# VectorE's column copies begin four steps behind ScalarE's

## The chip, the cores and the metric

The kernel runs on one core of one Trainium2 chip. The time is the device time of one execution in microseconds; the median of the runs counts. Engines: PE is TensorE, DVE is VectorE, ACT is ScalarE, POOL is GpSimd, SP is SyncE (it only issues transfers here).

## What is computed

One layer of a graph network with 12500 nodes of 64 features and 200000 edges, which are sorted by target:

```python
nodes = concat(x[src], x[dst])                       # per edge, 128 features
gates = (ssp(edge_attr @ We1 + be1) @ We2 + be2) * soft_cutoff(distance)
h = ssp(nodes @ Wn1 + bn1) @ Wn2 + bn2
message_sum = zeros_like(x).at[dst].add(h * gates)
x = layernorm(2 * x + ssp(message_sum @ Ws1 + bs1) @ Ws2 + bs2)
```

`ssp(x)` is softplus less log 2.

## The kernel before

**Steps.** The edges are cut into 391 steps of 512 (NG tiles `xg`, each with four parts of 128 edges, one edge per partition). Iteration i of the main loop is written out by hand as one order per engine:

- SP loads edge features (`eT`, every second step) and two windows of rows of a table of target features (`wns`) for step i+5.
- POOL gathers the source rows of step i+3: one indirect transfer per part of 128 rows (L204), four per step, into one of eight buffers `xg`. The gather after the eighth has to wait until PE's scatter of the buffer's former step is done, so POOL's group for a step starts on a signal of PE.
- PE: bias of layer 1 (L299) and layer 2 (L342), the scatter of step i-2 (L371, a product with one-hot columns), the transposes of step i+1 (L286), the edge part of layer 1 (L304), its node part (L311), and then layer 2 of step i (L349, L354).
- ACT copies the transposed tile (`xT`, L294), which L311 needs, then does columns (below), exp (L325) and log (L328).
- DVE adds the scatter's two windows to the sums (L391), multiplies `h` (L363) and the message (L367), takes the softplus' other half (L333), makes the one-hot columns of step i+3 (L280), and then does columns.

In a step whose gather group (of step i+5) has four parts, PE also does a product that nobody reads (L337, from `four`), before it waits for ACT's copy.

**Slots.** A copy of x lies transposed in SBUF (`xh`). For some of the parts of 128 edges, called slots, the source rows aren't gathered: an engine copies the column of each of the 128 sources (L262, 4 bytes in each partition), 16 in each step, into a tile `column`. DVE has queue 0 and part 1 of its tile, ACT queue 1 and part 2. After eight steps a tile is whole. `choose` then merges it on DVE: two instructions (L274) take the half of the partitions that holds the source, and PE adds the result to layer 1 with two products (L314) two steps later. In the `xg` of a slot's step the part is set to zero by DVE (L202, in iteration g-3, ahead of the windows), and POOL has three gathers instead of four. `slots_by_columns` places the slots: the first step that leaves enough steps for the copies and has no slot in the step before or behind; ACT's slots are placed first. `read_columns` loads 16 places into registers (L245) in each step; `columns` also has SP broadcast the slot's sources (`side`, L259) in the first of its eight steps.

**Node blocks.** When all edges of 512 nodes have been added (a first block of 212 nodes and 24 of 512; `block_steps` fixes the step from the shares of edges), the block's part is done beside the main loop, one piece per step: L410 is its first product. It stands in PE's order behind layer 2 of its iteration, reads the sums, and so waits for DVE's windows of that iteration; what DVE does after them is L425 and L426. Most blocks have L410 two iterations behind their step (`BLOCK_STEPS`): iterations 55, 98, 127, 151, 171, 189, 205, 220, 234, 247, 260, 272, 283, 294, 305, 315, 325, 334, 344, 353, 361, 370, 378, 386; the last block is done behind the loop.

## Time and profile before

| | us |
|---|---|
| median of 3 runs | 2354.7 (2352.55 to 2364.48) |
| profiled execution | 2351.35 |
| its span, first to last instruction | 2349.3 |
| mean granted clock of TensorE | 0.964 |
| DVE's column copies (6016) | 486.4 |
| ACT's column copies (6016) | 608.8 |
| merges L274 (188) | 53.5 |
| POOL's gathers L204 (1469) | 1391.3 |

A row of the page's groups gives the line, the engine, the operation, output and inputs, the shape, the count, then busy time and the mean of one in ns, and the idle time of the engine just before with what ended it. A row of the table of waits reads: who waited, for whom; microseconds in total, times, longest. A row of a timeline gives start, duration, engine, line, operation, operands and count, and in brackets the idle time before it and its releaser. A row of a stretch gives its limits and length, busy time and count of PE, PE's weight loads, DVE, ACT and POOL, the granted clock, and DMA share and rate.

### The profile page before, as it was taken

Reading aid. Unit: us, or ns where it says so; the run is one execution under the profiler, and the core shown is the slowest. Engines: PE = TensorE matmul, PEld = TensorE weight load, DVE = VectorE, ACT = ScalarE, POOL = GpSimd, SP = SyncE. Lnnn points to the kernel's source line nnn. Section 1 sums busy time; section 2 is a strip of 40 time slices with the busy share of each in tenths; the row PEclk is TensorE's granted clock in tenths of the full one; section 3 lists DMA queues with packets and bytes.
Section 4 is the critical chain, followed back from the end, with each engine's and each line's share of the span. In section 5 each row is a group of like instructions: output and inputs, shape, how many; then the busy total and the mean of one; then the engine's idle time right before and its main releaser. Section 6 shows DMA issues by size and latency. Waiting matters only on the chain.

```text
span 2349.3 us, 49245 instructions
## 1 busy us (share of the span) xinstructions
PE 1986.8 (85%) x12011; PEld 1549.9 (66%) x12011; DVE 1536.7 (65%) x9110; ACT 1511.8 (64%) x7412; POOL 1391.5 (59%) x1473
## 2 busy tenths in 40 slices
PE   6788888888888888888888888888888888888877
PEld 4676666666666666666666666666666666666665
DVE  4467666666666666666666667666666676667655
ACT  3466667666666666666667667666666666666653
POOL 6556666566666566666656566665666665556550
PEclk8799999999999999999999999999999999999988
DMA  6332232322222222222222222222222222222220
GB/s 190 95 83 71 64 70 57 79 62 74 60 59 57 54 62 54 59 56 61 55 58 63 52 61 63 59 59 58 59 59 59 59 61 60 55 56 59 60 51 13
DMA packets 162385, 149.51 MB, mean 64 GB/s; under 512 B 40564, under 2 KB 112021, under 8 KB 161962
## 3 DMA queue, kind: packets, MB, share of 16 engines
q1 hardware_dynamic: 114650, 96.55, 15.1%
q0 software_dynamic: 47008, 48.23, 10.9%
q8 instruction: 101, 1.65, 0.3%
q14 instruction: 192, 1.57, 0.2%
q10 hardware_dynamic: 434, 1.50, 0.2%
HBM read 136.50 MB, written 9.62 MB: 62 GB/s over the span
## 4 chain that ended last, share of the span: by engine, by line
PE 76%; issue 12%; DVE 6%; ACT 2%; DVEq 2%; another core or an unknown queue 1%; DMA 1%; POOL 0%; ACTq 0%; POOLq 0%
PE z L311 17%; PE gh L354 13%; PE z L371 10%; PE tx L286 9%; PE gh L349 8%; PE z L304 6%; PE z L337 4%; PE gh L342 3%; PE z L299 3%; DVE column L262 2%; DVEq L245 2%; ACT xT L294 1%; PE tx L410 1%; PE z L314 1%
## 5 line engine op out<-in xcount | busy, mean ns | idle before, releaser
L204 POOL DMA_INDIRECT xg<-in_x,src_i x1469 | 1391.3, 947 | 905.6 <-PE tx L286 378.3
L294 ACT COPY xT<-tx 106x512 f32<-106x512 f32 x391 | 228.6, 585 | 736.1 <-PE tx L286 704.6
L311 PE MATMUL z<-xT,wns 106*128 106x256 f32 x1564 | 464.1, 416 | 270.5 <-issue 238.0
L262 ACT COPY column<-xh 128x4 uint8 x6016 | 608.8, 193 | 0.0
L311 PEld LDWEIGHTS z<-xT,wns 106*128 106x128 f32 x1564 | 273.8, 197 | 420.4 <-issue 336.4
L262 DVE COPY column<-xh 128x4 uint8 x6016 | 486.4, 199 | 11.9 <-issue 6.9
L363 DVE TENSOR_TENSOR h<-gh,cut 128x256 f32<-128x256 f32 x391 | 166.0, 425 | 380.3 <-PE tx L286 260.8
L354 PE MATMUL gh<-consts,s 128*128 128x64 f32 x3128 | 400.2, 272 | 0.0
L354 PEld LDWEIGHTS gh<-consts,s 128*128 128x128 f32 x3128 | 389.6, 196 | 0.1
L328 ACT ACTIVATE u<-u,one 128x768 f32<-128x768 f32 x392 | 365.8, 933 | 13.5 <-ACT u L325 0.8
L333 DVE SCALAR_TENSOR_TENSOR s<-u,z 128x768 f32<-128x768 f32 x392 | 369.3, 942 | 0.4 <-issue 0.3
L391 DVE TENSOR_TENSOR sums<-sums,z 64x42 f32 x778 | 149.4, 192 | 325.5 <-issue 243.1
L325 ACT ACTIVATE u<-z 128x768 f32<-128x768 f32 x392 | 314.7, 803 | 47.2 <-PE z L311 25.5
L371 PEld LDWEIGHTS z<-xg,msg 128*128 128x128 f32 x1556 | 208.9, 195 | 140.9 <-issue 123.4
L371 PE MATMUL z<-xg,msg 128*128 128x84 f32 x1556 | 269.9, 297 | 13.6 <-DVE msg L367 13.5
L349 PEld LDWEIGHTS gh<-consts,s 128*128 128x128 f32 x1564 | 218.8, 196 | 92.7 <-DVE s L333 68.3
L349 PE MATMUL gh<-consts,s 128*128 128x128 f32 x1564 | 269.8, 296 | 11.8 <-issue 7.2
L286 PE MATMUL tx<-consts,xg 128*106 128x128 f32 x1564 | 243.9, 280 | 0.0
L304 PE MATMUL z<-eT,consts 128*128 128x256 f32 x782 | 243.7, 395 | 0.0
L286 PEld LDWEIGHTS tx<-consts,xg 128*106 128x106 f32 x1564 | 187.1, 145 | 1.2 <-issue 1.2
L367 DVE TENSOR_TENSOR msg<-gh,h 128x256 f32<-128x256 f32 x391 | 165.9, 424 | 13.4
L342 PE MATMUL gh<-row,ones 3*128 3x512 bf16 x391 | 149.3, 382 | 0.0
(107 smaller groups left out, 1193.4 us busy)
## 6 DMA issues: line engine op xcount, KB each, us to landing
eT<-in_eT SPq DMA_DIRECT2D x195, 256.0 KB
xg<-in_x,src_i POOLq DMA_INDIRECT x1469
wns<-table SPq DMA_DIRECT2D x782, 21.0 KB
table<-tb SPq DMA_DIRECT2D x14, 448.0 KB
side<-in_sides SPq DMA_DIRECT2D x94, 64.0 KB
y<-in_x SPq DMA_DIRECT2D x24, 128.0 KB
out<-y SPq DMA_DIRECT2D x24, 128.0 KB
xh<-in_xh SPq DMA_DIRECT2D x2, 781.5 KB
```

Source lines behind the costliest of these rows:

```text
L204: behind(note(("gather", g), nc.gpsimd.indirect_dma_start(out=xg[:, k, :D], out_offset=None, in_=x, in_offset=bass.IndirectOffsetOnAxis(ap ...
L262: copy(column_tiles[slot].bitcast(U8)[:, 4 * r : 4 * r + 4], xh[:, bass.ds(column_at[queue][j] - xh_at, 4)])
L286: ins = nc.tensor.transpose(tx[:, k, :], xgs[g][:, k, :DW], ident)
L294: note(("xcopy", g), nc.scalar.copy(xT, xTs[g]))
L304: nc.tensor.matmul(zs[g][:, 0, :HE], we1.rearrange("a h d -> a (h d)"), eTs[g], start=False, stop=True, skip_group_check=True)
L311: nc.tensor.matmul(zn, wns[:, g % REST, h, :], xTs[g][:, h], start=True, stop=not chosen, skip_group_check=True)
L325: nc.scalar.activation(us[g][:, part], z_of(g)[:, part], AF.Exp)
L328: nc.scalar.activation(us[g][:, part], us[g][:, part], AF.Ln, bias=one)
L333: nc.vector.scalar_tensor_tensor(ss[g].rearrange("p i t e -> p (i t e)")[:, part], us[g][:, part], BIG, z_of(g)[:, part], OP.min, OP.max)
L349: nc.tensor.matmul(v[:, 0, t], ss[g][:, 0, t, :], we2, start=False, stop=False, skip_group_check=True)
L354: nc.tensor.matmul(ghs[g][:, 1, 2 * t + h, :], ss[g][:, 1 + h, t, :], wn2, start=False, stop=h == 1 and t == 1, skip_group_check=True)
L371: ins = nc.tensor.matmul(sc, msgs[g][:, 2 * t : 2 * t + 2, :].rearrange("p h f -> p (h f)"), xgs[g][:, 2 * t : 2 * t + 2, D:DW], start=t = ...
```

## The change

Where the copies begin becomes a pair, for DVE and for ACT. ACT's still begin in iteration 8, DVE's in iteration 12 instead of 8.

```diff
-COLUMNS_FROM = 8
+COLUMNS_FROM = (12, 8)
...
-            if (g - 3 - COLUMNS_FROM + 1) * columns >= (n + 1) * P and not {g - 1, g, g + 1} & taken:
+            if (g - 3 - COLUMNS_FROM[queue] + 1) * columns >= (n + 1) * P and not {g - 1, g, g + 1} & taken:
...
-        return len(own[queue]) * P - columns_done[queue] if i >= COLUMNS_FROM else 0
+        return len(own[queue]) * P - columns_done[queue] if i >= COLUMNS_FROM[queue] else 0
```

ACT's 47 slots stay at steps 18, 26, ... 386. DVE's were at 20, 28, ... 388 (47) and are now at 22, 30, ... 382 (46). DVE's tiles become whole in iterations 19, 27, ... (remainder 3 of 8) instead of 15, 23, ... (remainder 7), where ACT's still do. The zeroing L202 of DVE's slots moves from iterations of remainder 1 to remainder 3. The rows below are in each engine's program order.

DVE, from message 167 to the windows of iteration 168 (remainder 0), before:

```order
L367 TENSOR_TENSOR msg<-gh,h 128x256
L333 TENSOR_SCALAR s<-u,z 128x768
L280 TENSOR_TENSOR xg<-consts,rel 128x4x42
L245 TENSOR_LOAD columns_at
L262 COPY column_24233<-xh 128x4 x16
L274 TENSOR_SCALAR chosen_25313<-side_24127,column_24126 64x128 x2
L274 TENSOR_SCALAR chosen_25316<-side_24234,column_24233 64x128 x2
L391 ISA
L391 TENSOR_TENSOR sums<-sums,z 64x42
```

and now (the two rows of L274 were the merges of ACT's and of DVE's slot):

```order
L367 TENSOR_TENSOR msg<-gh,h 128x256
L333 TENSOR_SCALAR s<-u,z 128x768
L280 TENSOR_TENSOR xg<-consts,rel 128x4x42
L245 TENSOR_LOAD columns_at
L262 COPY column_24638<-xh 128x4 x16
L274 TENSOR_SCALAR chosen_25118<-side_23929,column_23928 64x128 x2
L391 ISA
L391 TENSOR_TENSOR sums<-sums,z 64x42
```

ACT's merges stand alone there now; DVE's stand four iterations later, at the same place of the row.

DVE, from the columns of iteration 170 to the windows of iteration 171, a block's iteration (L410 on PE waits for these windows), before:

```order
L280 TENSOR_TENSOR xg<-consts,rel 128x4x42
L245 TENSOR_LOAD columns_at
L262 COPY column_25446<-xh 128x4 x16
L391 ISA
L391 TENSOR_TENSOR sums<-sums,z 64x42
```

and now:

```order
L280 TENSOR_TENSOR xg<-consts,rel 128x4x42
L245 TENSOR_LOAD columns_at
L262 COPY column_24638<-xh 128x4 x16
L202 MEMSET xg 128x64
L391 ISA
L391 TENSOR_TENSOR sums<-sums,z 64x42
```

The zeroing of a slot's part has come ahead of the windows.

DVE, from the columns of iteration 219 to the windows of iteration 220, another block's, before:

```order
L280 TENSOR_TENSOR xg<-consts,rel 128x4x42
L245 TENSOR_LOAD columns_at
L262 COPY column_32807<-xh 128x4 x16
L391 ISA
L391 TENSOR_TENSOR sums<-sums,z 64x42
```

and now, with the two merges of DVE's slot ahead of the windows:

```order
L280 TENSOR_TENSOR xg<-consts,rel 128x4x42
L245 TENSOR_LOAD columns_at
L262 COPY column_31990<-xh 128x4 x16
L274 TENSOR_SCALAR chosen_33085<-side_31991,column_31990 64x128 x2
L391 ISA
L391 TENSOR_TENSOR sums<-sums,z 64x42
```

Nothing else on DVE's row has moved between these rows.

## The prediction

> **What bounds the kernel now.** I read the page first, then the table of waits, then the timeline of POOL and of ACT's xT copy over a few steps.

> ```profile
> span 2349.3 us, 49245 instructions
> PE 1986.8 (85%) x12011; PEld 1549.9 (66%) x12011; DVE 1536.7 (65%) x9110; ACT 1511.8 (64%) x7412; POOL 1391.5 (59%) x1473
> ACT xT L294 <- PE tx L286: 704.6, 364, 9.8
> POOL xg L204 <- PE tx L286: 378.3, 284, 3.4
> ```

> No engine is full. ACT's copy waits for the transposes in nearly every step (364 waits of 391, 1.9 us each), POOL in most (284), and PE's layer 1 needs that copy. So the kernel is a ring of waits, and its length has to be read from single steps. POOL's gathers, then the xT copies of the same stretch:

> ```profile
> 1002.88 0.94 POOL L204 DMA_INDIRECT xg<-in_x,src_i  x1 [0.91 <-PE tx L286]
> ...
> 1006.63 0.94 POOL L204 DMA_INDIRECT xg<-in_x,src_i  x1 [0.30 <-issue]
> 1008.91 0.94 POOL L204 DMA_INDIRECT xg<-in_x,src_i  x1 [1.33 <-PE tx L286]
> ...
> 1013.55 0.94 POOL L204 DMA_INDIRECT xg<-in_x,src_i  x1 [1.21 <-PE tx L286]
> ...
> 1019.59 0.94 POOL L204 DMA_INDIRECT xg<-in_x,src_i  x1 [1.35 <-PE tx L286]
> ```

> ```profile
> 1008.73 0.58 ACT L294 COPY xT<-tx 106x512 f32<-106x512 f32 x1 [2.19 <-PE tx L286]
> 1013.44 0.58 ACT L294 COPY xT<-tx 106x512 f32<-106x512 f32 x1 [0.93 <-PE tx L286]
> 1019.41 0.59 ACT L294 COPY xT<-tx 106x512 f32<-106x512 f32 x1 [2.20 <-PE tx L286]
> 1025.46 0.58 ACT L294 COPY xT<-tx 106x512 f32<-106x512 f32 x1 [2.27 <-PE tx L286]
> ```

> A group of four gathers lasts 6.03 us from its start to the next group's (1002.88 to 1008.91), a group of three, which is a step whose tile has a slot, 4.64 (1008.91 to 1013.55). The copies come in the same rhythm: 4.71, 5.97, 6.05. The last gather ends 1.16 us before the copy (1006.63 + 0.94 to 1008.73). Thus **a step's length is set by how many gathers POOL has in it**, 4 or 3, and each slot is worth about 1.39 us. DVE's and ACT's column copies and the merges lie inside these steps.

> **The change part by part.**

> *Slots.* ACT's stay where they are (tiles 18, 26, 34 ... 386, 47 of them). DVE's go from 20, 28 ... 388 (47) to 22, 30 ... 382 (46). Every eight steps still hold two groups of three and six of four, now four apart. Their sum doesn't change: 2 x 4.7 + 6 x 6.0 either way. A group that is ready early gains nothing either, since POOL's first gather of a group waits for PE in every step above. What is lost is the slot of tile 388. Its group of three is the one that starts at 2279.54, in the last dozen steps, where a step is longer:

> ```profile
> 2279.54 0.94 POOL L204 DMA_INDIRECT xg<-in_x,src_i  x1 [3.38 <-PE z L371]
> ```

> ```profile
> 2271.68 0.59 ACT L294 COPY xT<-tx 106x512 f32<-106x512 f32 x1 [0.16 <-PE tx L286]
> 2280.16 0.58 ACT L294 COPY xT<-tx 106x512 f32<-106x512 f32 x1 [4.70 <-PE tx L286]
> 2285.97 0.58 ACT L294 COPY xT<-tx 106x512 f32<-106x512 f32 x1 [1.85 <-PE tx L286]
> ```

> With four gathers that step took 8.48 (2271.68 to 2280.16), with three 5.81. So the lost slot costs 1.4 (mid-kernel) to 2.7 us (here); I take the nearer row, **+2.7**.

> *Merges.* Four of them stood together, at the end of DVE's every eighth step:

> ```profile
> 1022.33 0.58 DVE L274 SCALAR_TENSOR_TENSOR chosen<-side,column 64x128 f32<-64x128 int32 x2
> 1023.82 0.59 DVE L274 SCALAR_TENSOR_TENSOR chosen<-side,column 64x128 f32<-64x128 int32 x2 [0.91 <-DVE chosen L274]
> 1024.55 0.19 DVE L391 TENSOR_TENSOR sums<-sums,z 64x42 f32 x1
> 1025.26 0.20 DVE L391 TENSOR_TENSOR sums<-sums,z 64x42 f32 x1 [0.52 <-issue]
> 1025.49 0.42 DVE L363 TENSOR_TENSOR h<-gh,cut 128x256 f32<-128x256 f32 x1
> ```

> They take 2.08 us with their gap (1022.33 to 1024.41), the windows follow, and h starts at 1025.49, when PE's signal for it had come at the latest (ACT's copy, which waits for a later PE instruction, starts at 1025.46). That step is 6.05 long, no longer than its neighbours: the merges just fit under the gathers, and if they grew, the cover would be gone. Halving them frees about 1 us of DVE that nothing waits for. Only the step behind a short one may gain: 5.97 where DVE is on time, 6.05 with DVE late. That is at most 0.08 in each of 46 rounds of eight, -3.7 us, and at least 0; I take the middle, **-2**.

> *DVE's copies.* 128 copies, 2 merges and 8 register loads fewer on DVE, 4 matmul rows fewer on PE, one gather more:

> ```profile
> L262 DVE COPY column<-xh 128x4 uint8 x6016 | 486.4, 199 | 11.9 <-issue 6.9
> ```

> 128 of the 6016 copies are 10.3 us of DVE time (486.4 / 47), all of it beside gathers: 0, and at best the 0 to 1 us that DVE might be late with in the last steps. The side tiles' transfers on SP's queue are the same, now in two steps of eight; SP issues them behind the step's own loads, and no wait of the table is for them: 0.

> *Where the moved pieces meet a node block.* This is the one place where DVE's lateness is paid. PE's first matmul of a block (L410) stands before the step's scatter and transposes and waits for DVE's windows; whatever DVE has in front of those windows, a memset of a slot's tile or the merges, delays PE. Three such meetings: without either, with a memset, behind four merges.

> ```profile
> 1041.06 1.10 PE L410 MATMUL tx<-sums,consts 128*128 128x256 f32 x4 [0.20 <-issue]
> ```

> ```profile
> 923.45 0.11 DVE L202 MEMSET xg<- 128x64 f32 x1
> 923.49 0.13 DVE L391 TENSOR_TENSOR sums<-sums,z 64x42 f32 x1
> 924.87 0.20 DVE L391 TENSOR_TENSOR sums<-sums,z 64x42 f32 x1 [1.26 <-issue]
> ```

> ```profile
> 925.22 1.10 PE L410 MATMUL tx<-sums,consts 128*128 128x256 f32 x4 [1.54 <-DVE sums L391]
> ...
> 1625.52 1.36 PE L410 MATMUL tx<-sums,consts 128*128 128x256 f32 x4 [1.77 <-DVE sums L391]
> ```

> ```profile
> 920.52 0.58 ACT L294 COPY xT<-tx 106x512 f32<-106x512 f32 x1 [0.92 <-PE tx L286]
> 928.84 0.58 ACT L294 COPY xT<-tx 106x512 f32<-106x512 f32 x1 [4.55 <-PE tx L286]
> ...
> 1620.56 0.59 ACT L294 COPY xT<-tx 106x512 f32<-106x512 f32 x1 [2.03 <-PE tx L286]
> 1629.59 0.58 ACT L294 COPY xT<-tx 106x512 f32<-106x512 f32 x1 [5.26 <-PE tx L286]
> ```

> Alone, PE waits 0.20 us. Behind a memset the second window stalls 1.26, PE waits 1.54, and the step is 8.32 long (920.52 to 928.84), 2.3 over a step of four gathers. Behind four merges PE waits 1.77 and the step is 9.03 (1620.56 to 1629.59), 3.0 over. Part of that is the clock: after the stall the granted clock of TensorE falls.

> ```profile
> 922.90:926.30 3.40, 1.86 (x12) 1.36 (x12) 0.92 (x11) 1.36 (x2) 1.89 (x2) 1.00 0.20 43
> 926.50:929.90 3.40, 3.40 (x14) 2.83 (x13) 3.37 (x18) 1.06 (x8) 1.37 (x2) 0.50 0.06 16
> ```

> With PE busy for 1.86 of 3.40 us, the next 3.4 us ran at 0.50 of full speed. [...]

> Now the counting, with the blocks' plan laid beside the slots (a block's first matmul stands two steps behind the step that its edges are complete in, which the code fixes). A block's first matmul stands at steps 171, 283, 315 (remainder 3 of 8), where a memset now comes in front; at 305 and 361 (remainder 1), where it goes away; at 220 and 260 (remainder 4), where two merges now stand in front; at 272 and 344 (remainder 0), where four become two. So three meetings begin and two end at a memset, price 0 to 2.3, I take 1.4, near the middle: net +1.4. Two begin at two merges, 0 to 3.0, I take 0.8 (half of the 1.57 by which PE's wait behind four merges, 1.77, is over the clean 0.20): +1.6. Two shrink by as much: -1.6. Blocks that meet a short step lose its gain: four did, four do. Sum **+1.4**, an estimate from these rows, with ends of -7.8 (two memsets gone at 2.3 each, two blocks relieved by 1.6 each) and +12.9 (3 x 2.3 + 2 x 3.0).

> Sum: 2.7 - 2 + 1.4 = +2.1 us against the profiled execution's 2351.35 (span 2349.3), 2353.5. The median of the runs shown, 2354.7, lies 3.35 above that execution, so as a median I expect 2354.7 + 2.1 = **2357**, to the microsecond. A measurement of this kernel can tell some 0.5% (12 us) from no change.

> **The rivals.**

> *Only the lost slot counts.* The steps are bound by gathers, everything else is covered: +1.4 to +2.7, 2356 to 2357. For it: merges and copies wait for nothing in most steps. It ends where the forecast does.

> *Slower: the moved pieces trip the clock at node blocks.* Place: PE's L410 at steps 171, 283, 315 (memset) and 220, 260 (merges). Price: if each costs as much as the worst quoted, the 12.9 above, with nothing given back at the others, and +2.7: 2354.7 + 15.6 = 2370. It decides once DVE's second window ends so late that PE stands for about 1.5 us, as in the row of 925.22; 0.20 costs nothing. For it: DVE had no slack there (924.87). Against: the same number of such meetings goes away.

> *Faster: four merges in one step were what made DVE late.* Behind them stands the 9.03 step, and DVE's rows from 1022.33 show it just in time. If halving saves the 3.0 at both blocks of remainder 0 and at one more place like them (-9.0), all of the -3.7, and nothing begins elsewhere, the sum is 2.7 - 12.7 = -10, 2345; with a whole stall of 2.3 saved elsewhere too, 2342. Against: most rounds show no cost.

> *The spacing itself gains.* If POOL could use the four steps between short groups to run ahead, 30 gathers of 1.25 us (1.24 from start to start inside a group) would need 37.5 us where eight steps take 45.7. Every group's start waits for PE, 1.2 to 1.35 us after the gather before, so I give this almost nothing: it would be 2354.7 - 8.2 x 46 = 1977.

> **How the numbers follow.** Forecast 0.45 and only the lost slot 0.29, both within 0.5%; clock trips 0.15, all of it beyond 0.5%; relief 0.10, half of it below 2343, which is 0.5% under the median; running ahead 0.01. Range: the ends of the three terms are 1.4 - 3.7 - 7.8 = -10 and 2.7 + 0 + 12.9 = +16, 2344 to 2370; cut by the rarer half of each side, 2346 to 2368. Slower by over 0.5% (above 2366.5): 0.15; faster 0.05 + 0.01 = 0.06; same the rest, 0.79.

> **What would show it.** Groups of three gathers of 4.64 us four steps apart, groups of four still 6.03; the step of 8.48 / 5.81 at the end twice near 8.5; L274 in pairs with no late h; PE's waits for DVE's windows at L410 up at the three blocks with a memset in front, down at 305 and 361. I am wrong if a group of four gets shorter or longer than 6.0, or if the granted clock falls in more than two or three stretches that are new.

## The result, and the profile after

| | before | after |
|---|---|---|
| median, runs of both on one chip | 2355.76 us (22 runs) | 2368.12 us (22 runs) |
| ratio of the times, 95% interval | | 1.005 [1.0035, 1.0064] |
| profiled execution | 2351.35 us | 2367.95 us |
| its span | 2349.3 us | 2366.2 us |
| mean granted clock of TensorE | 0.964 | 0.962 |

The change made the kernel slower by 0.35 to 0.64%, 12.4 us between the medians. I had forecast +2.1 us. By the ratio this is 2366.5 us on the prediction's base of 2354.7, inside the range of 2346 to 2368; the median itself, 2368.12, stands on the range's upper edge. So about 10 us are to be explained. First the changed kernel's page and two rows of its table of waits:

```profile
span 2366.2 us, 49082 instructions
PE 1993.2 (84%) x12011; PEld 1554.2 (66%) x12011; DVE 1528.2 (65%) x8979; ACT 1516.5 (64%) x7412; POOL 1397.0 (59%) x1474
ACT xT L294 <- PE tx L286: 708.4, 367, 10.3
POOL xg L204 <- PE tx L286: 381.7, 284, 4.7
```

The work of the engines is the same within 9 us, and each of the two waits grew by less than 4 us in total. The averages don't show the loss, so I went back to single steps. POOL's group starts in the changed kernel, from its timeline:

```profile
604.40 0.95 POOL L204 DMA_INDIRECT xg<-in_x,src_i  x1 [1.34 <-PE tx L286]
...
610.48 0.94 POOL L204 DMA_INDIRECT xg<-in_x,src_i  x1 [1.38 <-PE tx L286]
...
616.52 0.94 POOL L204 DMA_INDIRECT xg<-in_x,src_i  x1 [1.35 <-PE tx L286]
...
621.16 0.95 POOL L204 DMA_INDIRECT xg<-in_x,src_i  x1 [1.20 <-DVE sums L391]
```

Groups of four last 6.08 and 6.04 us, a group of three 4.64 (616.52 to 621.16). An undisturbed round of eight steps costs what it did before. I call a step with three gathers short and one with four long. ACT's xT copies cut the whole span into stretches; these are the copies that begin steps 19, 94, 376 and 390, before:

```profile
154.89 0.59 ACT L294 COPY xT<-tx 106x512 f32<-106x512 f32 x1 [2.18 <-PE tx L286]
...
587.29 0.59 ACT L294 COPY xT<-tx 106x512 f32<-106x512 f32 x1 [0.94 <-PE tx L286]
...
2233.03 0.58 ACT L294 COPY xT<-tx 106x512 f32<-106x512 f32 x1 [1.78 <-PE tx L286]
...
2326.94 0.59 ACT L294 COPY xT<-tx 106x512 f32<-106x512 f32 x1
```

and after:

```profile
155.11 0.59 ACT L294 COPY xT<-tx 106x512 f32<-106x512 f32 x1 [1.91 <-PE tx L286]
...
598.22 0.59 ACT L294 COPY xT<-tx 106x512 f32<-106x512 f32 x1 [0.90 <-PE tx L286]
...
2251.72 0.59 ACT L294 COPY xT<-tx 106x512 f32<-106x512 f32 x1 [2.37 <-PE tx L286]
...
2343.07 0.59 ACT L294 COPY xT<-tx 106x512 f32<-106x512 f32 x1
```

| stretch | before | after | difference |
|---|---|---|---|
| to step 19 | 154.9 | 155.1 | +0.2 |
| steps 19 to 93 (the table's chunks are made beside) | 432.4 | 443.1 | **+10.7** |
| steps 94 to 375 | 1645.7 | 1653.5 | +7.8 |
| steps 376 to 389 | 93.9 | 91.4 | -2.6 |
| step 390 to the end of the span | 22.4 | 23.1 | +0.8 |

The differences add up to the 16.9 us between the spans. (That is more than the 12.4 between the medians: the profiled execution of before was 4.4 us faster than its median, that of after stood at its median.) Most of it lies in a stretch that the prediction didn't look at and that holds one node block. There the changed kernel has short steps that are no longer short. Step 65 is one; the copies that begin steps 64 to 67, and the granted clock in stretches around it:

```profile
423.61 0.59 ACT L294 COPY xT<-tx 106x512 f32<-106x512 f32 x1 [1.51 <-PE tx L286]
429.74 0.59 ACT L294 COPY xT<-tx 106x512 f32<-106x512 f32 x1 [2.19 <-remote]
437.62 0.59 ACT L294 COPY xT<-tx 106x512 f32<-106x512 f32 x1 [3.20 <-PE tx L286]
443.61 0.59 ACT L294 COPY xT<-tx 106x512 f32<-106x512 f32 x1 [0.82 <-PE tx L286]
```

```profile
427.00:430.20 3.20, 1.79 (x13) 1.53 (x12) 1.17 (x5) 1.01 (x3) 1.47 (x3) 1.00 0.51 139
430.30:433.70 3.40, 3.32 (x12) 2.96 (x12) 3.30 (x24) 2.73 (x19) 2.46 (x3) 0.50 0.19 39
433.80:440.40 6.60, 6.60 (x26) 5.41 (x26) 4.02 (x25) 2.73 (x19) 2.79 (x3) 0.50 0.26 66
```

PE was busy for 1.79 of 3.20 us, then ran for 10 us at a granted clock of 0.50 (a dip, from here on). Step 65 has three gathers and lasted 7.88 us (429.74 to 437.62), 3.2 too long, and the long step behind it gave almost nothing back (5.99). Before the change there were dips in this stretch as well. Here is one in the long step 75 of the kernel before, copies and stretches:

```profile
478.69 0.58 ACT L294 COPY xT<-tx 106x512 f32<-106x512 f32 x1 [2.15 <-PE tx L286]
484.90 0.58 ACT L294 COPY xT<-tx 106x512 f32<-106x512 f32 x1 [1.54 <-PE tx L286]
490.75 0.58 ACT L294 COPY xT<-tx 106x512 f32<-106x512 f32 x1 [1.90 <-PE tx L286]
```

```profile
476.00:479.30 3.30, 2.11 (x14) 1.54 (x13) 1.48 (x7) 1.15 (x5) 1.58 (x3) 1.00 0.12 22
479.40:482.80 3.40, 3.40 (x13) 3.04 (x13) 2.31 (x19) 2.72 (x17) 2.49 (x4) 0.50 0.14 32
```

That dip of 3.4 us made a step of 6.21 and one of 5.85, nothing in sum: at full clock PE stands still for 1.15 us of a long step (4.89 busy of 6.04 in this row of the changed kernel), and the slow products run into that time.

```profile
610.30:616.34 6.04, 4.89 (x30) 3.73 (x30) 3.54 (x24) 3.75 (x19) 3.78 (x4) 1.00 0.30 72
616.34:621.04 4.70, 4.06 (x27) 3.35 (x28) 3.75 (x24) 3.75 (x19) 2.84 (x3) 1.00 0.16 35
```

A short step leaves 0.64 (4.06 of 4.70). Counted over steps 19 to 375 from the records of the granted clock, the dips didn't become more frequent (18 before, 16 after; 85 and 99 us in all). What changed is where they lie: 3.6 us of the half-speed time were in short steps before, 53.4 are now.

About half of the 10.7 us lies in one place, steps 24 and 25. These copies begin steps 24, 25 and 26 after the change:

```profile
184.05 0.59 ACT L294 COPY xT<-tx 106x512 f32<-106x512 f32 x1 [2.13 <-PE tx L286]
192.14 0.59 ACT L294 COPY xT<-tx 106x512 f32<-106x512 f32 x1 [4.15 <-remote]
200.02 0.59 ACT L294 COPY xT<-tx 106x512 f32<-106x512 f32 x1 [2.28 <-PE tx L286]
```

The two steps take 8.09 and 7.88 us, together 5.2 over the medians of their kinds; before the change they were 0.4 under. PE stood for 3.43 us ahead of its layer 1 at 192.78, and a dip of 10.2 us that began at 191.34 lay on step 25, which is now short. Every trace with slots four apart but that of the last run has this stop (2.4 to 5.9 us over the two steps), and none with slots two apart (-0.4 to 0.0). What starts it isn't known.

### The profile page after: what moved, and what is told of

It reads as the page before. It is cut to its first block, busy times and chain, and to the rows that moved or that the text cites. A ratio compares the mean times of both kernels' runs of the same rounds, so it can differ in the third digit from the quotient of the medians.

```text
span 2366.2 us, 49082 instructions
## 1 busy us (share of the span) xinstructions
PE 1993.2 (84%) x12011; PEld 1554.2 (66%) x12011; DVE 1528.2 (65%) x8979; ACT 1516.5 (64%) x7412; POOL 1397.0 (59%) x1474
## 4 chain that ended last, share of the span: by engine, by line
PE 73%; issue 12%; DVE 5%; ACT 2%; DVEq 2%; another core or an unknown queue 0%; ACTq 0%
PE z L311 16%; PE gh L354 12%; PE z L371 9%; PE tx L286 8%; PE gh L349 8%; PE z L304 6%; PE z L337 3%; PE gh L342 3%; PE z L299 3%; DVEq L245 2%; DVE column L262 1%; PE tx L410 1%; ACT xT L294 1%; DVE h L363 1%; PE z L314 1%
## 5 line engine op out<-in xcount | busy, mean ns | idle before, releaser
L204 POOL DMA_INDIRECT xg<-in_x,src_i x1470 | 1396.7, 950 | 917.0 <-PE tx L286 381.7
L294 ACT COPY xT<-tx 106x512 f32<-106x512 f32 x391 | 229.3, 586 | 750.1 <-PE tx L286 708.4
L262 ACT COPY column<-xh 128x4 uint8 x6016 | 612.3, 195 | 0.0
L262 DVE COPY column<-xh 128x4 uint8 x5888 | 476.0, 198 | 11.9 <-issue 7.5
L363 DVE TENSOR_TENSOR h<-gh,cut 128x256 f32<-128x256 f32 x391 | 166.1, 425 | 405.2 <-PE tx L286 328.9
L328 ACT ACTIVATE u<-u,one 128x768 f32<-128x768 f32 x392 | 366.6, 935 | 12.7
L391 DVE TENSOR_TENSOR sums<-sums,z 64x42 f32 x778 | 149.7, 192 | 344.9 <-issue 228.5
L371 PEld LDWEIGHTS z<-xg,msg 128*128 128x128 f32 x1556 | 209.0, 195 | 141.3 <-issue 124.3
L371 PE MATMUL z<-xg,msg 128*128 128x84 f32 x1556 | 269.8, 297 | 13.1 <-DVE msg L367 11.5
L286 PE MATMUL tx<-consts,xg 128*106 128x128 f32 x1564 | 243.4, 280 | 0.0
L286 PEld LDWEIGHTS tx<-consts,xg 128*106 128x106 f32 x1564 | 186.5, 145 | 0.9 <-issue 0.9
```

What stands on the lines that cost most here:

```text
L204: behind(note(("gather", g), nc.gpsimd.indirect_dma_start(out=xg[:, k, :D], out_offset=None, in_=x, in_offset=bass.IndirectOffsetOnAxis(ap ...
L262: copy(column_tiles[slot].bitcast(U8)[:, 4 * r : 4 * r + 4], xh[:, bass.ds(column_at[queue][j] - xh_at, 4)])
L286: ins = nc.tensor.transpose(tx[:, k, :], xgs[g][:, k, :DW], ident)
L294: note(("xcopy", g), nc.scalar.copy(xT, xTs[g]))
L328: nc.scalar.activation(us[g][:, part], us[g][:, part], AF.Ln, bias=one)
L371: ins = nc.tensor.matmul(sc, msgs[g][:, 2 * t : 2 * t + 2, :].rearrange("p h f -> p (h f)"), xgs[g][:, 2 * t : 2 * t + 2, D:DW], start=t = ...
```

## The experiments

Ratios are to the kernel before, timed on the same chip as the kernel in question (the changed kernel itself wasn't timed on these four chips); its medians there were 2388.35 us (the first four), 2389.22 (the next four), 2392.11 (the next three) and 1947.45 (the last). "Excess" is a step's length over the median of its kind (short or long) in the same trace.

**Which part of the change costs.** My first theory was a wait at node blocks: the zeroing L202, now ahead of the windows at blocks 171, 283 and 315. Four kernels, each with one part.

Lost slot, on the kernel before:

```diff
-        for g in range(NG - 2):
+        for g in range(NG - 2 - 8 * (queue == 0)):
```

> The kernel before with DVE's last slot (tile 388) left out, nothing moved. If the lost slot is the cause of most of the change, 10 us or more over the kernel before. If the slots' new places are the cause, only what one gather costs, 1.4 to 2.7 us, ratio 1.001. If the merges' new places are the cause, the same 1.001.

Measured: 1.0004 [0.9985, 1.0022], about +1 us. The interval, -3.6 to +5.3 us, can't tell 0 from the 2.7 that I gave the slot, but the slot isn't worth the 10 us.

Merges apart, slots as before:

```diff
-COLUMNS_FROM = 8
+COLUMNS_FROM = (10, 8)
```

> DVE's copies begin in iteration 10: its slots stay at 20, 28 ... 388 (all 47, two behind ACT's), only its merges move out of ACT's iteration, to remainder 1. If the merges' separation is what costs (merges in front of more node blocks), 6 us or more slower than before. If the slots' new places are the cause, no change or a little faster, ratio 0.997 to 1.001.

Measured: 1.0007 [0.9989, 1.0025]. Two merges and two merges cost what four in one step cost, to within 0.3%.

Slots apart, with all merges in one step as before:

```diff
-        return len(own[queue]) * P - columns_done[queue] if i >= COLUMNS_FROM[queue] else 0
+        return len(own[queue]) * P - columns_done[queue] if i >= min(COLUMNS_FROM) else 0
```

> DVE's slots at 22, 30 ... 382 as in the change, but its copies begin in iteration 8, so that all four merges stand together as before. If the slots' new places (zeroing and short steps) are the cause, as slow as the change, ratio 1.004 to 1.006. If the merges' places are the cause, 1.001.

Measured: 1.0091 [1.0058, 1.0124]. With the slots at their new places the loss is there also when all four merges stand together.

Zeroing behind the windows, in the changed kernel:

```diff
-                nc.vector.memset(xg[:, k, :D], 0.0)
+                if g < AHEAD:
+                    nc.vector.memset(xg[:, k, :D], 0.0)
                 continue
...
                 at(onehot, i + 3)
+                if i >= 0:
+                    at(zero, i + AHEAD)
```

> The change, with the zeroing of a slot's part behind the one-hot columns instead of ahead of the windows. If the zeroing that now stands ahead of the windows at blocks 171, 283 and 315 and elsewhere makes DVE late and PE's clock fall, most of the 12 us comes back or more, ratio 0.996 to 1.001 to the kernel before. If the short steps' places alone are the cause (a late clock can't hide in a short step), it stays at 1.004 to 1.006.

Measured: 1.0047 [1.0024, 1.0069]. In its trace the three blocks have no excess left (0.0, 0.1 and 0.2 us, where the changed kernel had 0.3, 4.0 and 2.4 over four steps), but the time is still that of the changed kernel. The theory of the zeroing falls.

**Merges or places?** Next I took the merges directly ahead of a short step for the cause (theory A), against the slots' places as such (B).

Copies two iterations earlier, slots as in the change:

```diff
 COLUMNS_FROM = (12, 8)
+COPIES_FROM = (10, 6)
...
-        return len(own[queue]) * P - columns_done[queue] if i >= COLUMNS_FROM[queue] else 0
+        return len(own[queue]) * P - columns_done[queue] if i >= COPIES_FROM[queue] else 0
```

> The changed kernel with its slots where they are (g = 18, 22, 26, 30, ...), but the byte copies of both engines begun two iterations earlier (10 and 6 instead of 12 and 8), so that a pair of merges falls into iterations i = 1 and 5 (mod 8) and a step between the merges and the short step behind them is long. Nothing else moves; the start, with the load of xh, is two iterations less covered. Theory A (a short step costs more when the merges, which delay VectorE, stand directly ahead of it; a long step has slack for them): the loss goes, ratio to the kernel before 1.000 to 1.002, and the excess of the steps j = 1 and 5 (mod 8) falls from some 25 and 14 us to under 10 each. Rival B (the short steps' new places cost by themselves, because the node blocks' halts meet them): ratio stays 1.004 to 1.007 and the excess stays at j = 1 and 5.

Measured: 1.0082 [1.0051, 1.0113]. Against A. (Its profiled execution, 2387.64 us, was the fastest of its seven runs, the others took 2404 to 2417, so its trace doesn't show this loss.)

Each merge one iteration later:

```diff
+    ready = [0]
     def choose(pool):
-        while whole:
+        for _ in range(ready[0]):
...
+        ready[0] = len(whole)
```

> The changed kernel with each pair of merges issued one iteration later, so that they fall behind the short step instead of ahead of it (i = 0 and 4 mod 8). Theory A (merges directly ahead of a short step make it late): ratio 1.000 to 1.002. Rival B (the slots' places meet the node blocks): 1.004 to 1.007, as the changed kernel.

Measured: 1.0896 [1.0854, 1.0938], which neither theory gave. The edit made a new wait: PE's product with the merged columns (L317 here) is issued in the next iteration and now stands waiting for the merge (L276). PE and DVE in one such step, then the copies that begin it and the next:

```profile
681.93 0.70 PE L314 MATMUL z<-xT,wns 106*128 106x256 f32 x2 [0.24 <-ACT xT L297]
684.86 0.49 PE L317 MATMUL z<-chosen,wn_twice 128*128 128x128 f32 x2 [2.22 <-issue]
```

```profile
684.23 0.58 DVE L276 SCALAR_TENSOR_TENSOR chosen<-side,column 64x128 f32<-64x128 int32 x2
```

```profile
681.30 0.59 ACT L297 COPY xT<-tx 106x512 f32<-106x512 f32 x1 [0.93 <-PE tx L289]
688.57 0.59 ACT L297 COPY xT<-tx 106x512 f32<-106x512 f32 x1 [0.98 <-PE tx L289]
```

PE stands for 2.22 us and this step takes 7.27. Where half speed follows the stop it is more: over the kernel these steps have medians of 10.1 and 9.3 us, and the mean granted clock is 0.868. It says nothing about A and B, but it shows how little separates the merges from PE: one iteration.

All four merges ahead of a short step, in the kernel before:

```diff
-        return len(own[queue]) * P - columns_done[queue] if i >= COLUMNS_FROM else 0
+        return len(own[queue]) * P - columns_done[queue] if i >= COLUMNS_FROM - 2 else 0
```

> The kernel before with its slots where they are (18, 20, 26, 28, ...), but the copies of both engines begun at iteration 6 instead of 8, so that all four merges stand directly ahead of the short step j = 7 (mod 8) instead of ahead of the long step j = 1. Theory A (merges ahead of a short step make it late): slower, 1.003 to 1.009, the excess of j = 7 growing by 8 to 20 us. Rival B (places of the slots alone count): 0.998 to 1.002.

Measured: 1.0079 [1.0051, 1.0108], as A had it: with the slots at their old places, merges at the wrong distance cost as much as the change. Over steps 19 to 375 the short step's remainder 7 has an excess of 25.1 us and the step behind it 24.0 (8.9 and 7.2 in the trace of before). Its trace also has more dips than that of before, 28 against 18, with 171 us of half speed against 85.

The whole pattern two iterations later:

```diff
-COLUMNS_FROM = (12, 8)
+COLUMNS_FROM = (14, 10)
```

> The changed kernel with both engines' columns begun two iterations later still (14 and 10): slots 20, 24, 28, 32, ..., merges at i = 1 and 5 (mod 8), again directly ahead of the short steps, now j = 3 and 7 (mod 8); the last slot but one is lost, worth 0 to 1.4 us. Theory A (merges ahead of a short step): as the changed kernel, 1.004 to 1.007. Rival B (node blocks' halts fall on other steps than before): the meetings are dealt anew, so the time moves away from the changed kernel's, most likely back to 0.999 to 1.003.

Measured: 1.0085 [1.0054, 1.0115]. The loss followed the slots: the excess sits at remainders 3 and 7 now (25.4 and 21.5 us). That speaks against an accident of where node blocks fall.

**Dips.** Both theories had looked at remainders. When I listed every dip by its step, a third one came out (C): in steps 26 to 93, away from the node block there, dips begin in any kind of step, but those that meet a short step cost. A dip of 3.4 us that begins in a short step takes 1.06 to 1.14 us from the two steps that it touches (11 cases in eight traces), in a long step with a long one behind it -0.1 to 0.2. One of 6.8 us takes 1.5 to 2.4 when it begins in a short step (seven cases), -0.1 to 2.2 otherwise (13 cases). One of 10.2 us reaches beyond its step and takes 2.7 to 3.1 when it begins in a short one, 1.5 to 4.1 otherwise (five cases), so for these the kind of the step makes no clear difference.

| kernel | slots | dips begun in short steps | in long steps | excess of steps 26 to 93, us |
|---|---|---|---|---|
| before | 2 and 6 apart | 0 | 6 | 4.2 |
| lost slot | 2 and 6 apart | 1 | 7 | 9.5 |
| merges apart | 2 and 6 apart | 1 | 6 | 3.2 |
| all merges ahead of a short step | 2 and 6 apart | 3 | 5 | 9.9 |
| after | 4 apart | 3 | 2 | 10.1 |
| slots apart | 4 apart | 5 | 3 | 11.6 |
| zeroing late | 4 apart | 4 | 2 | 10.1 |
| copies early | 4 apart | 2 | 5 | 9.9 |
| pattern later | 4 apart | 5 | 1 | 12.2 |
| no merges | 4 apart | 4 | 5 | 10.1 |

One step in four is short. These are single traces, and the excess of one can mislead (the lost slot's 9.5 goes with a ratio of 1.0004); the counts add up over the kernels. With slots four apart 23 of 41 dips begin in one, with slots two apart 5 of 29. And behind step 92 most dips go with a node block's first product: up to step 375 ten of 12 before and eight of nine after begin within 2.2 us of an L410. From step 92 on PE also does the filler product L337, which is left out while the table's chunks are made. So the tests were to take away the merges, and to put the filler in.

No merges at all, in the changed kernel:

```diff
-            chosen_columns[g, k] = pool.tile([P, P], F32, name=f"chosen{queue}", bufs=2)
-            for h, op in enumerate((OP.is_lt, OP.is_ge)):
...
+            chosen_columns[g, k] = column_tiles[slot]
```

> The changed kernel without its merges: the product of a slot reads the copied columns as they are (so the node terms of these slots are wrong and 186 small VectorE instructions of 0.28 us are gone); copies, side transfers, slots and zeroings stay. Theory C (in steps up to 91 a pair of merges makes VectorE late enough to trip the clock, and since the change the dip falls on a short step, which has no slack): the excess of steps 19 to 93, 15.4 us in the changed kernel and 4.2 in the kernel before, falls to under 6, and the ratio to 0.994 to 1.001. Rival B (four steps between slots cost by themselves): the excess stays over 11 and the ratio at 1.004 to 1.008.

Measured: 0.9995 [0.9975, 1.0015], the time that C gave, but not by its way: nine dips are still there in steps 26 to 93 and the excess of steps 19 to 93 is 15.8 us. So it isn't the merges that trip the clock there, and this part of C falls. Over steps 19 to 375 its trace has 45 us of half speed in short steps, nearly the 53 of the changed kernel, and the stop at step 24 too, and still it is no slower than the kernel before: half speed in short steps doesn't make the loss by itself. Where their removal saves the time the trace doesn't show, and the kernel before wasn't tried without merges, so how much of it belongs to the change stays open.

The filler from the start on, in the changed kernel:

```diff
-                if c is None and four(i + AHEAD + BEHIND - 3):
+                if four(i + AHEAD + BEHIND - 3):
```

> The changed kernel with its filler product (128x256, issued so far from step 92 on) also in the long steps before, beside the table's chunks; nothing of the result changes. Theory C (dips of the clock that merges trip only where the filler is missing): excess of steps 19 to 93 from 15.4 to 3 to 8 us, ratio 0.997 to 1.002. Rival B (spacing by itself), or dips that the filler doesn't prevent: ratio 1.004 to 1.008, or more, as PE gets some 40 products of 0.38 us more.

Measured: 1.0005 [0.9984, 1.0026]; with the filler the changed kernel is as fast as the kernel before, to within 0.3%. In steps 26 to 93 away from the block no dip is left, and the excess of steps 26 to 93 fell from 10.1 to 4.8 us. (Over steps 19 to 93 it is 10.9; the rest is a stop at step 24, which the fillers don't reach.) Step 65 again, the copies that begin it and the next two:

```profile
429.69 0.58 ACT L294 COPY xT<-tx 106x512 f32<-106x512 f32 x1 [2.33 <-remote]
434.41 0.58 ACT L294 COPY xT<-tx 106x512 f32<-106x512 f32 x1 [0.80 <-PE tx L286]
440.61 0.58 ACT L294 COPY xT<-tx 106x512 f32<-106x512 f32 x1 [1.78 <-PE tx L286]
```

4.72 us instead of 7.88. In the stretch that holds PE's wait PE is now busy for 2.50 of 3.40 us, where it was 1.79 of 3.20, and the clock stays at 1.00:

```profile
428.50:431.90 3.40, 2.50 (x14) 1.62 (x13) 2.72 (x13) 2.21 (x18) 1.73 (x2) 1.00 0.40 119
```

Two things stay open here. The filler wasn't tried alone in the kernel before, so it may be a gain that has nothing to do with the change and only makes up for it. And the excess that went away in steps 19 to 93, 4.5 us, is less than half of the 0.45% (about 11 us) by which the ratio fell.

The kernel before with this filler and two more ahead of L410:

```diff
+            if filler:
+                for _ in range(2):
+                    nc.tensor.matmul(z[:, HE:], we1.rearrange("a h d -> a (h d)"), consts[:, :HE], start=True,
+                                     stop=True, skip_group_check=True)
...
-                if c is None and four(i + AHEAD + BEHIND - 3):
+                if four(i + AHEAD + BEHIND - 3):
```

> The kernel before with the same early filler, and with two more filler products ahead of a node block's first product (L410), which keep PE busy while it waits for VectorE's windows. Theory C, with the node blocks as the place of most of the rest of the excess (31 us of 39 in the kernel before): the early excess stays at 3 to 5 us and that of the node blocks falls by 10 to 30 us, ratio 0.988 to 0.996. Against it: the two products run for 0.76 us whether PE would have waited or not, and where the wait is longer than they are the clock falls all the same: ratio 0.998 to 1.006.

Measured: 0.9933 [0.9908, 0.9959], faster than the kernel before by 10 to 22 us. Five dips are left in steps 19 to 375, with 31 us of half speed (the kernel before, in its trace on another chip: 18 and 85).

The changed kernel with the same fillers was to show whether the change still costs when there are few dips:

> The changed kernel with both kinds of filler: the early one beside the table's chunks and the two ahead of a node block's first product. The kernel before with the same fillers took 0.9933 of the kernel before. Theory D (the change costs time only through dips of the clock that fall on short steps; the fillers leave few dips): the change no longer matters, 0.990 to 0.996, within 0.002 of the other. Rival B (spacing, or the meeting of node blocks with short steps, costs at full clock as well): 0.997 to 1.000, the other's figure and the 0.005 of the change.

Measured: 1952.74 us, 1.0024 [1.0015, 1.0034]. It can't answer its question. On the chip of this run the kernel before took 1947.45 us, 17 to 19% less than elsewhere, and this kernel's trace has no dip at all between steps 19 and 375. The last section shows what differs there. So whether the change costs anything at full clock on the other chips stays open; the 0.0024 here holds the change and the fillers together.

## Why the prediction was wrong by 10 us

The range held, but partly by luck: its upper end was made of stops at five node blocks, and most of the loss came from a stretch for which the prediction had no term.

- **Rhythm of the steps**: right. 6.04 to 6.08 and 4.64 us, the sum of an undisturbed round unchanged, no running ahead of POOL.
- **Lost slot, +2.7**: too large by the trace; the time of the kernel with the slot alone taken away, 1.0004, can't tell. The three copies around the place in the changed kernel show no step of 8.5:

```profile
2290.28 0.59 ACT L294 COPY xT<-tx 106x512 f32<-106x512 f32 x1 [0.51 <-PE tx L286]
2298.20 0.59 ACT L294 COPY xT<-tx 106x512 f32<-106x512 f32 x1 [4.12 <-PE tx L286]
2304.80 0.59 ACT L294 COPY xT<-tx 106x512 f32<-106x512 f32 x1 [1.85 <-PE tx L286]
```

  7.92 and 6.60, where it was 8.48 and 5.81: 0.2 us more in sum. With a fourth gather the slot's own step took 6.60, not 8.48, so the step that I read the price off was long for another reason.
- **Merges, -2**: no gain to be seen; the time with the merges alone apart, 1.0007 [0.9989, 1.0025], can't exclude 2 us. The pairs run under the gathers, as said, and h follows the windows without a gap in the short step that ends at 621.04 of the changed kernel:

```profile
620.04 0.29 DVE L274 SCALAR_TENSOR_TENSOR chosen<-side,column 64x128 f32<-64x128 int32 x1 [0.49 <-issue]
620.75 0.41 DVE L391 TENSOR_TENSOR sums<-sums,z 64x42 f32 x2 [0.41 <-issue]
621.18 0.42 DVE L363 TENSOR_TENSOR h<-gh,cut 128x256 f32<-128x256 f32 x1
```

- **Node blocks, +1.4**: the mechanism was there. At 283 PE waited as long as the quoted meeting had it, and the step was 8.45 (1707.74 to 1716.19):

```profile
1712.48 1.10 PE L410 MATMUL tx<-sums,consts 128*128 128x256 f32 x4 [1.55 <-DVE sums L391]
```

```profile
1707.74 0.59 ACT L294 COPY xT<-tx 106x512 f32<-106x512 f32 x1 [2.27 <-PE tx L286]
1716.19 0.59 ACT L294 COPY xT<-tx 106x512 f32<-106x512 f32 x1 [4.65 <-PE tx L286]
1722.86 0.59 ACT L294 COPY xT<-tx 106x512 f32<-106x512 f32 x1 [0.33 <-PE tx L286]
```

  The step behind it is short and took 6.67 (to 1722.86), 2.0 too long: the dip lay on it (half speed from 1713.68 to 1720.51). I had counted one step for each meeting, and "four did, four do" for the blocks that meet a short step. Over four steps the three blocks had 6.7 us of excess where I had put 4.2. The 21 blocks from 98 to 370 rose from 31.4 to 37.5, though at 171 a memset in front cost next to nothing and at 305 and 361 its going away gave about 1.0 each. The count of the meetings had left one out: 353 also has remainder 1, and the memset ahead of its windows goes away too (PE's wait fell from 2.92 to 2.12 us, the block's excess from 3.0 to 1.7). With it three meetings begin and three end, and by the prediction's own prices the term is 0 instead of +1.4. And at 127, 151 and 247, where nothing that DVE has ahead of the windows had moved but the second step of the four is now short, the excess rose from 2.6, 1.6 and 0.9 to 4.0 each, 6.9 us that no term had.
- **The step that failed** is the sentence that opens that part: "This is the one place where DVE's lateness is paid." Steps 19 to 93, with one block, hold 10.7 of the 16.9 us between the two traces, and the prediction had put nothing there. About half of it is the stop at steps 24 and 25. In the steps behind it the clock also falls away from the node block, where the filler is missing: dips that begin in the short steps 45, 65 and 89 took 1.7, 3.1 and 1.1 us, and one of 10.2 us that began in the long step 60 took 4.1. That it is DVE's lateness which trips the clock there isn't shown; without any merge the dips were still there. The prediction would have needed a list of every dip, with the kind of the step under it; the rows for the dips before the change were in the trace of before.
- **The rival "moved pieces trip the clock"** gave nearly the right time, 2370, and part of the mechanism: its five blocks (171, 283, 315, 220, 260) rose by 8.7 us in the traces where it had 12.9. But other blocks fell by about as much, and with the zeroing out of the way at three of the five the time stayed at 1.0047. The sign that I had named, the clock falling in more than two or three new stretches, did come: ten of the 16 dips after the change lie more than one step from any dip of before, though the number of dips fell from 18 to 16.

Shown by times: kernels with the slots' new places took 1.0047 to 1.0091 of the kernel before (1.0091, 1.0047, 1.0082 and 1.0085), kernels with the lost slot or the merges apart alone 1.0004 and 1.0007, and merges at a wrong distance can cost as much at the old places (1.0079). Shown in the traces: a dip of 3.4 us costs about 1 us more when it begins in a short step, and the stop at step 24 goes with slots four apart. Argued only: that these dips make up the loss, why they begin in short steps more often when slots stand four apart, and that the filler's 1.0005 is the loss of the change taken away rather than a gain of its own. Two results fit no single account: with merges two iterations earlier the time is 0.8% above the kernel before with the slots at either place, and no merges at all brought the changed kernel to 0.9995.

## What to carry to other kernels

When a change moves short steps about, ask which steps absorb a stall: lay the dips of the granted clock over the steps, and see which kind each one meets, before and after, also in the stages that the change isn't about. A product that nobody reads, put where PE waits, can be worth more than its price where PE isn't the bound (0.9933 here). And a slack that is not used in the steady state pays for disturbances: 1.15 us of it took up a dip of 3.4 us, 0.64 didn't.

## What the runs showed of the hardware

```profile
257.49:260.90 3.41, 1.96 (x11) 1.38 (x10) 1.97 (x6) 1.77 (x15) 1.58 (x3) 1.00 0.30 91
260.90:264.31 3.41, 3.41 (x26) 2.93 (x26) 2.28 (x22) 2.60 (x8) 1.89 (x3) 1.00 0.15 31
```

**How soon ACT's copy follows the transposes differs between the traces.** In those of all runs but the last, ACT's copy starts 1.2 to 1.3 us (medians) after the end of POOL's last gather and, but for the kernel with the merges later, 1.0 to 1.3 us after the end of the last transpose; in the traces of before and after, 131 and 128 of the 391 copies start within 0.1 us of that end. The transposes for the copy at 610.30 in the changed kernel:

```profile
608.31 0.60 PE L286 MATMUL tx<-consts,xg 128*106 128x128 f32 x4
```

They end at 608.91, and the last gather ends at 609.09 (608.15 + 0.94):

```profile
608.15 0.94 POOL L204 DMA_INDIRECT xg<-in_x,src_i  x1 [0.30 <-issue]
```

In the last run, the changed kernel with fillers, transposes and copy stand like this:

```profile
898.58 0.60 PE L286 MATMUL tx<-consts,xg 128*106 128x128 f32 x4
```

```profile
899.21 0.59 ACT L294 COPY xT<-tx 106x512 f32<-106x512 f32 x1
903.77 0.59 ACT L294 COPY xT<-tx 106x512 f32<-106x512 f32 x1 [0.78 <-PE tx L286]
```

The copy starts 0.03 us after the transposes' end, while POOL is gathering, and most steps last 4.56 us (899.21 to 903.77) with three gathers or with four (4.78 at remainders 2 and 6): there PE is the bound, busy in all of this step and for 1760.3 of the 1785 us from 115 to 1900.

```profile
899.21:903.77 4.56, 4.56 (x31) 3.81 (x30) 3.90 (x24) 3.75 (x19) 3.34 (x5) 1.00 0.36 93
```

So a long step lasts as long as POOL's group of four (6.04 to 6.08 us) where the changed kernel was traced, and as long as PE's work (4.56) in the last run's trace, and a filler that paid on the former chips (0.9933) needn't pay on that of the last run. The kernel before was timed on both (2355.76 to 2392.11 us and 1947.45), but no program has a trace on both. What holds the copy back in the other traces isn't known from these runs; a gather takes 0.95 us on both.
